# Layer 2 of a four-layer image network: group statistics from one product, shorter chains, and a reordered boundary turn

## The chip, the core and the metric

The kernel runs on one core of a Trainium2 chip. A core has five engines with queues of their own, each in order: TensorE (PE, matrix products and transposes, result in PSUM), VectorE (DVE), ScalarE (ACT), GpSimd (POOL) and SyncE (SP, which here issues all DMAs). They wait for each other through semaphores. The metric is the device time of one execution in microseconds (us), lower is better.

## The reference

Sixteen images of 64 x 64 tokens with 256 channels pass four layers, each `x + layer(group_norm(x))`. All numbers are 32-bit floats. What matters here:

```python
def _gn(v, G=32, eps=1e-5):              # statistics over a whole image and 8 channels
    g = v.reshape(B_, H_, W_, G, C_ // G)
    m = jnp.mean(g, axis=(1, 2, 4), keepdims=True)
    s = jnp.var(g, axis=(1, 2, 4), keepdims=True)
    return ((g - m) / jnp.sqrt(s + eps)).reshape(v.shape)

# layer 1, in part: two maps (mean and max over channels) and a 7x7 convolution of them
feat = jnp.concatenate([jnp.mean(xc, -1, keepdims=True), jnp.max(xc, -1, keepdims=True)], -1)
s = lax.conv_general_dilated(feat, lsa_w, (1, 1), 'SAME', ...)

# layer 2: an involution, 3x3, 16 groups of weights made from the input itself
r = relu(((x @ Wr + br) - mean) * rsqrt(var + BN_EPS) * gamma + beta)
w = (r @ Ws + bs).reshape(B, H, W, G, KK)[:, :, :, :, None, :]
xi = x @ Wi + bi
xp = jnp.pad(xi, ...)
patches = stack of the 9 shifted copies of xp, reshaped to (B, H, W, G, F // G, KK)
out = jnp.sum(w * patches, axis=-1)

x = x + _L0_conv_ref(_gn(x), ...)        # linear attention
x = x + _L1_conv_ref(_gn(x), ...)        # gates, scan over tokens, batch norm
x = x + _L2_conv_ref(_gn(x), ...)        # involution 3x3
x = x + _L3_conv_ref(_gn(x), ...)        # involution 7x7
```

The group norm ahead of layer 2 needs the mean and variance of the finished layer 1 of an image, and the one ahead of layer 3 those of the finished layer 2.

## The kernel before

The program has three large stages, one for each of layers 0, 2 and 3, and between the first two a scan (layer 1) and a pass for the batch norm's statistics. Channels lie on the partitions, in two halves of 128; an image is cut into 8 chunks of 512 tokens.

**Layer 0** runs over pairs of image and head half, 8 steps each, `n` from 0 to `LAST + 15`; the 16 steps from `LAST` on only drain the pipeline. An automatic scheduler sets the order of instructions on each engine there. In the drain the last image gets its gate (`gate1`, at its end L508 on PE, L512 on ACT, L513 to L517 on DVE), then `mapped` is called for its 8 chunks: `affine` scales a chunk (one half on ACT, L172, one on DVE, L175), eight transposes put it into PSUM (L526, tile `px`, two buffers), and DVE reduces it twice, maximum (L530) and sum (L531). After the maps, DVE builds the convolution's band matrices from the 98 weights (L695, L702, then 14 copies, L709, into `convT`) and PE multiplies them with the maps (`psc`, L718), before the scan begins.

**Layer 2** is a loop of 152 turns (`TURNS`, L1286) whose order on every engine is written by hand (`manual_schedule`). Four jobs run in it, each behind the one before by a fixed number of turns, `LAG = (0, 13, 21, 32)` (L1285): the end of layer 1 for a chunk (`end_of_layer1`: DVE `z` L1058, ACT relu L1067 with sums, POOL add L1071, ACT squares L1078), the projection into the padded image `pad` (`projected`, PE L1124, ACT L1128; after chunk 7 two copies L1135 and L1136 fill the halo line), the involution for four lines, and the centring for layer 3 (`centred`, POOL L857). So the first 21 turns have no involution, and the last 3 have only what follows it.

In one turn with an involution, DVE does `z` and `pf` for another chunk (L1058), then two products `pd` of patches and weights (L1208) and one reduction (L1383). POOL reduces the first product (L1221, L1222). PE does, in this order: weights `pw` (L1155), `pr` of the next chunk (L1145), the addition of the finished sums to the residual `lo` (L1195), nine pairs of transposes `pt` for the next turn's patches `xs` (L1170, each pair evicted by ACT, L1174; after three of them `between` is called), the next residual (L1186), transposes of the finished output (L1234), and the projection (L1124). A **boundary turn**, once for each image, prepares chunk 0 of the next image; there the projection of chunk 7 is placed ahead of `pr`, since all nine pairs of chunk 0 read the image that it completes.

Between these jobs run **chains**, one link at each call of `step()`, three calls in a turn: at the start, in `between`, and between the two products. `norm2` and `norm3` are such chains. Each calls `group_norm`, whose `moments` turns the 8 partial sums and squares of each channel into mean and variance with six small DVE instructions (L113 to L123); a product with `gmat` averages means over groups of 8 channels (`pg`, L134), DVE copies it (L140, L142), three instructions form the deviations (L146 to L148), a second product averages them (`pv`, L151), and L93 (DVE) and L94 (POOL) make the inverse root. `norm2` then scales the layer's weights by it on ACT (`wrs`, `wis`, L1096), multiplies them with the means (`pm`, L1106, PE), and forms two biases on DVE (`b` L1112, `bis` L1114). `norm3` ends with the means spread over all partitions (`pb` L844, copy `gmb` L849). With its empty links `norm2` takes four turns, and its last link, the biases, is at the third call of `step()` in a boundary turn, so in DVE's order between the two products.

SP issues in each turn the loads of the next one, then the stores of the last, then the centring's load. A load or store waits in SP's queue until its tile is free or full.

Of the kernel before, what the change touches and what calls it, by code (L numbers as in the profile page):

```python
# [9 lines left out]
F32 = mybir.dt.float32  # L10
AF = mybir.ActivationFunctionType
# [25 lines left out]
def network(ctx: ExitStack, tc: tile.TileContext, a: dict, out: bass.AP):  # L37
# [33 lines left out]
    mean1 = gconst("mean1", [P, NI, 2])  # L71
# [37 lines left out]
    def moments(mv, sums, squares, base, shift):  # L109


        t = small.tile([P, 4], F32, tag="mom", name="mom")
        nc.vector.tensor_reduce(t[:, 0:2], sums, AX.X, ALU.add)  # L113
        nc.vector.tensor_reduce(t[:, 2:4], squares, AX.X, ALU.add)
        if base is None:
            nc.vector.tensor_scalar(mv[:, :, 0], t[:, 0:2], 1.0 / NT, None, ALU.mult)
        else:
            nc.vector.scalar_tensor_tensor(
                mv[:, :, 0], t[:, 0:2], 1.0 / NT, base, ALU.mult, ALU.add
            )  # L120
        nc.vector.tensor_tensor(t[:, 0:2], mv[:, :, 0], shift, ALU.add)
        nc.vector.tensor_tensor(t[:, 0:2], t[:, 0:2], t[:, 0:2], ALU.mult)
        nc.vector.scalar_tensor_tensor(  # L123
            mv[:, :, 1], t[:, 2:4], 1.0 / NT, t[:, 0:2], ALU.mult, ALU.subtract
        )

    def group_norm(fill, stats, pool, tag, apart=False, kept=None, negated=None, beside=None):
# [3 lines left out]
        fill(mv, *stats)  # L131
# [3 lines left out]
        if apart:  # L135
            yield
        gm, rstd = kept or [
# [3 lines left out]
        if negated is not None:  # L141
            nc.vector.tensor_scalar(negated, pg[:, 0:2], -1.0, None, ALU.mult)  # L142
        if apart:
            yield
# [7 lines left out]
        after = beside() if beside else None  # L152
        if apart:
            yield
        inv_sqrt(rstd, pv[:, 0:2], GN_EPS)
        if after:
            after()
        yield
        if apart:
            yield  # L160
# [19 lines left out]
    with ExitStack() as st:  # L180
# [71 lines left out]
        def norm0(i):  # L252
            _, gm, rstd = yield from group_norm(aggregated, (st0.pop(i),), sm, "sm")
            nb = small.tile([P, 2], F32, tag="gn_b", name="gn_b")
            nc.vector.tensor_tensor(nb, gm, rstd, ALU.mult)
            nc.vector.tensor_scalar(nb, nb, -1.0, None, ALU.mult)
            gn0[i] = (gm, rstd, nb)
# [225 lines left out]
        def gate1(i):  # L483

            mv, gm, rstd = yield from group_norm(aggregated, (st1.pop(i),), sm, "sm")
# [31 lines left out]
            nc.vector.tensor_copy(mean1[:, i, :], mv[:, :, 0])  # L517

        def mapped(i, ch):

            xc = loaded.pop(("xm", i, ch))
            affine(xc, xc, i)
# [6 lines left out]
            cols = slice(2 + ch * 4, 6 + ch * 4)  # L529
            nc.vector.tensor_reduce(maps[:, 1, i, cols], px, AX.X, ALU.max)  # L530
            nc.vector.tensor_reduce(maps[:, 0, i, cols], px, AX.X, ALU.add)  # L531
# [58 lines left out]
        for n in range(LAST + 16):  # L590
# [54 lines left out]
            for job in work:  # L645
                if job[0] == "xm":
                    mapped(*job[1:])
# [11 lines left out]
    with ExitStack() as st:  # L659
# [22 lines left out]
        convT = sconst("convT", [P, 5, 2, 2, HW])  # L682
        with tc.tile_pool(name="s_conv", bufs=1) as pcv:
            bmask = pcv.tile([P, 7, HW], F32, tag="bmask", name="bmask")
            nc.sync.dma_start(out=bmask, in_=a["bmask"])
            lsa = pcv.tile([P, 7, 7, 2], F32, tag="lsa", name="lsa")
            nc.sync.dma_start(
                out=lsa.rearrange("p i j c -> p (i j c)"), in_=a["lsa_w"].partition_broadcast(P)
            )
            band = pcv.tile([P, 7, 2, HW], F32, tag="band", name="band")  # L690
            term = pcv.tile([P, 7, 2, HW], F32, tag="term", name="term")
            for dj in range(7):
                dst = band if dj == 0 else term
                for c in range(2):
                    nc.vector.tensor_tensor(  # L695
                        dst[:, :, c, :],
                        lsa[:, :, dj, c].unsqueeze(2).broadcast_to([P, 7, HW]),
                        bmask[:, dj, :].unsqueeze(1).broadcast_to([P, 7, HW]),
                        ALU.mult,
                    )  # L700
                if dj:
                    nc.vector.tensor_tensor(band, band, term, ALU.add)  # L702
            nc.vector.memset(convT, 0.0)
            for delta in range(-2, 3):
                for rr in range(2):
                    for r2 in range(2):
                        di = 2 * delta + rr - r2 + 3
                        if 0 <= di < 7:
                            nc.vector.tensor_copy(  # L709
                                convT[rr * HW : (rr + 1) * HW, delta + 2, :, r2, :],  # L710
                                band[rr * HW : (rr + 1) * HW, di, :, :],
                            )

# [162 lines left out]
    with ExitStack() as st:  # L876
# [25 lines left out]
        mvb = bconst("mvb", [P, 2, 2])  # L902
        sb2 = folded(pc, "l2", "L2_mean", "L2_var", "L2_gamma", "L2_beta", "br")
# [143 lines left out]
        def end_of_layer1(i, rc):  # L1047

            if rc == 0:
                st0[i] = [  # L1050
# [110 lines left out]
        def patches(i, rc, between):  # L1161
# [3 lines left out]
            for j in range(3):  # L1165
# [9 lines left out]
                if j == 0:  # L1175
                    between()
# [589 lines left out]
```

## Time and profile before

| | us |
|---|---|
| median of 3 runs (lowest, highest) | 8064.9 (8053.64, 8065.29) |
| the profiled execution | 8044.92 |
| its span, first to last instruction | 8042.9 |

The profiled execution in stretches, in us from the start of its span; the columns of the engines are busy time, "clock" the share of full speed granted to TensorE, DMA the mean busy share of the 16 DMA engines:

| stretch | what runs | us | PE | DVE | ACT | POOL | clock | DMA |
|---|---|---|---|---|---|---|---|---|
| 0 to 3036 | layer 0 | 3036 | 2609.8 | 2261.3 | 1694.8 | 668.5 | 0.93 | 0.44 |
| 3036 to 3061 | maps of the last image | 25 | (see below) | | | | | |
| 3061 to 3167 | convolution of the maps, scan | 106 | 77.8 | 38.4 | 22.2 | 8.1 | 0.55 | 0.02 |
| 3167 to 3355 | batch norm's statistics | 188 | 145.5 | 177.0 | 172.3 | 0.7 | 0.96 | 0.97 |
| 3355 to 3476 | layer 2, turns without involution | 121 | (see below) | | | | | |
| 3476 to 5400 | layer 2, full turns | 1924 | (see below) | | | | | |
| 5400 to 5697 | layer 2, turns without `z` | 297 | 255.7 | 284.2 | 182.2 | 229.4 | 0.93 | 0.59 |
| 5697 to 5760 | last sums, constants and first loads of layer 3 | 63 | 27.4 | 5.0 | 15.0 | 12.4 | 0.53 | 0.71 |
| 5760 to 8043 | layer 3 | 2283 | 1981.7 | 1062.5 | 1276.4 | 455.8 | 0.98 | 0.82 |

A timeline line reads: start, duration, engine, source line, operation, out<-in with shapes, how many are merged, and in brackets the idle time of the engine before it and what ended that. Lines of layer 2's steady turns, from one start of L1383 to the next, give the length of a turn: 16.16 us where no chain has a link on DVE (4874.00 to 4890.16), 17.61 with `moments` of `norm2` (4800.12 to 4817.73), and 22.49 in a boundary turn (4851.51 to 4874.00). Eight turns, one image, take 141.5 us (4748.69 to 4890.16).

### The profile page before, as it was taken

Reading aid. Unit: us, or ns where it says so; the run is one execution under the profiler, and the core shown is the slowest. Engines: PE = TensorE matmul, PEld = TensorE weight load, DVE = VectorE, ACT = ScalarE, POOL = GpSimd, SP = SyncE. Lnnn points to the kernel's source line nnn. Section 1 sums busy time; section 2 is a strip of 40 time slices with the busy share of each in tenths; the row PEclk is TensorE's granted clock in tenths of the full one; section 3 lists DMA queues with packets and bytes.
Section 4 is the critical chain, followed back from the end, with each engine's and each line's share of the span. In section 5 each row is a group of like instructions: output and inputs, shape, how many; then the busy total and the mean of one; then the engine's idle time right before and its main releaser. Section 6 shows DMA issues by size and latency. Waiting matters only on the chain.

```text
span 8042.9 us, 214160 instructions
## 1 busy us (share of the span) xinstructions
PE 6914.4 (86%) x88876; PEld 5169.1 (64%) x88876; DVE 5726.5 (71%) x6802; ACT 4930.7 (61%) x11392; POOL 3050.4 (38%) x2155
## 2 busy tenths in 40 slices
PE   7888888888889976589999999999688888888898
PEld 5666666666666663156666666666577777777777
DVE  6777777777777776789999999999544444444444
ACT  3555555555555553877777777776455555555554
POOL 1222222222222210168888888887312122111112
PEclk9999999999999986899999999999899999999999
DMA  6644444444333333867878788875688888888887
GB/s 220 197 144 137 137 131 139 137 133 140 129 125 121 113 111 120 313 211 259 275 267 278 267 275 278 266 249 201 204 259 256 259 260 259 258 255 259 260 263 238
DMA packets 1075453, 1689.52 MB, mean 210 GB/s; under 512 B 136417, under 2 KB 680626, under 8 KB 1073330
## 3 DMA queue, kind: packets, MB, share of 16 engines
q1 hardware_dynamic: 1074482, 1675.83, 64.3%
q8 instruction: 700, 11.47, 0.6%
q14 instruction: 271, 2.22, 0.1%
HBM read 1228.47 MB, written 469.76 MB: 211 GB/s over the span
## 4 chain that ended last, share of the span: by engine, by line
PE 48%; DVE 23%; issue 11%; ACT 8%; DMA 7%; POOL 2%; SPq 1%; DVEq 0%; POOLq 0%; ACTq 0%
PE pk L1484 13%; PE pa L1550 8%; DVE pd L1208 7%; PE pkv L302 6%; PE py L444 5%; DVE x L1383 4%; PE pq L290 3%; DMA xn<-in_x 2%; PE pr L1451 2%; PE px L1124 2%; PE pt L1170 2%; PE pctx L368 2%; PE po L429 1%; DVE mq L403 1%; DVE x L472 1%
## 5 line engine op out<-in xcount | busy, mean ns | idle before, releaser
L1208 DVE TENSOR_TENSOR pd<-xs,pw 128x4608 f32<-128x4608 f32 x256 | 1261.4, 4947 | 6.4 <-POOL x L1222 4.5
L1484 PE MATMUL pk<-rt,span 64*128 64x176 f32 x12288 | 1170.5, 326 | 62.6 <-issue 55.3
L1494 ACT ACTIVATE wm<-pk,spanb 128x176 f32<-128x176 f32 x2560 | 847.3, 425 | 569.2 <-PE pk L1484 566.6
L1570 POOL TENSOR_TENSOR ex<-ex,rx 128x192 f32<-128x192 f32 (+2 forms) x768 | 437.1, 570 | 1800.8 <-DVE ex L1563 1272.4
L1221 POOL TENSOR_TENSOR pd<-pd 128x2048 f32<-128x2048 f32 (+2 forms) x384 | 1072.4, 2793 | 118.0 <-DVE pd L1208 65.2
L1484 PEld LDWEIGHTS pk<-rt,span 64*128 64x128 f32 x12288 | 959.8, 190 | 143.4 <-issue 85.5
L1563 DVE SCALAR_TENSOR_TENSOR ex<-pa,msk,ex 128x192 f32<-128x192 f32 x704 | 294.3, 418 | 1004.0 <-ACT ex L1562 925.2
L302 PE MATMUL pkv<-wq,xn 128*128 128x256 f32 x4096 | 983.0, 386 | 2.7 <-ACT va L311 1.9
L302 PEld LDWEIGHTS pkv<-wq,xn 128*128 128x128 f32 x4096 | 784.3, 195 | 228.1 <-issue 114.6
L1550 PE MATMUL pa<-wm,xw 126*32 126x48 f32 x45056 | 753.7, 215 | 200.8 <-issue 182.8
L1499 DVE TENSOR_TENSOR wm<-pk,spanb 128x704 f32<-128x704 f32 x896 | 794.0, 888 | 185.7 <-PE pk L1484 183.8
L398 POOL TENSOR_TENSOR qa<-qa,mq 128x1024 f32<-128x1024 f32 x256 | 501.6, 1980 | 1026.4 <-DVE mq L403 512.0
L1550 PEld LDWEIGHTS pa<-wm,xw 126*32 126x32 f32 x45056 | 623.4, 112 | 383.5 <-issue 334.5
L1170 PE MATMUL pt<-ident,pad 128*128 128x128 f32 x4608 | 639.1, 287 | 145.1 <-ACT xs L1174 87.6
L1170 PEld LDWEIGHTS pt<-ident,pad 128*128 128x128 f32 x4608 | 521.7, 146 | 302.4 <-ACT xs L1174 117.6
L1383 DVE TENSOR_REDUCE x<-pd 128x512 f32<-128x4608 f32 x128 | 634.0, 4953 | 4.4
L1174 ACT COPY xs<-pt 128x512 f32<-128x512 f32 x1152 | 588.9, 597 | 37.2 <-PE pt L1170 36.9
L444 PE MATMUL py<-wo,o 128*128 128x256 f32 x2048 | 542.4, 422 | 64.3 <-ACT va L311 59.6
L444 PEld LDWEIGHTS py<-wo,o 128*128 128x128 f32 x2048 | 496.0, 310 | 108.8 <-ACT va L311 76.7
L290 PE MATMUL pq<-xn,wq 128*128 128x512 f32 x1024 | 533.1, 637 | 33.4 <-ACT xn L165 21.1
L1562 ACT ACTIVATE ex<-pa,msk 128x192 f32<-128x192 f32 x704 | 300.2, 426 | 373.3 <-PE pa L1550 185.3
L1124 PE MATMUL px<-x2p,wis 128*128 128x512 f32 x1024 | 467.9, 599 | 11.8 <-DMA x2p<-x_d 8.1
(243 smaller groups left out, 11893.5 us busy)
## 6 DMA issues: line engine op xcount, KB each, us to landing
xw<-strips SPq DMA_DIRECT2D x1408, 256.0 KB
xn<-in_x SPq DMA_DIRECT2D x256, 512.0 KB
x_d<-x SPq DMA_DIRECT2D x256, 512.0 KB
strips<-cen SPq DMA_DIRECT2D x352, 256.0 KB
xin<-in_x SPq DMA_DIRECT2D x128, 512.0 KB
x<-in_x SPq DMA_DIRECT2D x128, 512.0 KB
xm<-x_d SPq DMA_DIRECT2D x128, 512.0 KB
x2p<-x_d SPq DMA_DIRECT2D x128, 512.0 KB
```

The costliest lines, as they stand in the source:

```text
L290: nc.tensor.matmul(pq, lhsT=wq[:, h, f0 : f0 + P], rhs=xn[:, h], start=(h == 0), stop=(h == 1),)
L302: nc.tensor.matmul(pkv[:, q], lhsT=xn[:, h, q * P : (q + 1) * P], rhs=wq[:, h, f0 + P : f0 + 384], start=(h == 0), stop=(h == 1),)
L444: nc.tensor.matmul(py[:, q, :], lhsT=om[i, hf][:, :, ch * 4 + q], rhs=wo[:, hf, :], start=(hf == 0), stop=(hf == 1),)
L1124: nc.tensor.matmul(px, lhsT=w[:, h, fh * P : (fh + 1) * P], rhs=x2[:, h], start=(h == 0), stop=(h == 1),)
L1170: nc.tensor.transpose(pt[:, k, h * P : (h + 1) * P], lines[:, h, rc * 4 + e + k, 2 * j : 2 * j + P], ident,)
L1208: nc.vector.tensor_tensor(pd.rearrange("p r (g f) k -> p r g f k", f=16), run, pw.rearrange("p r (g k) -> p r g k", k=9).unsqueeze(3).broa ...
L1221: nc.gpsimd.tensor_tensor(pd[..., 0:n], pd[..., 0:n], pd[..., n : 2 * n], ALU.add)
L1383: nc.vector.tensor_reduce(x3[:, :, P:C], pd1, AX.X, ALU.add)
L1484: nc.tensor.matmul(pkv[:, b, m], lhsT=span[half, first + gg, s0 : s0 + P], rhs=rto[half, o // 4 * 2 + m, :], start=True, stop=True,)
L1494: nc.scalar.activation(dst[:, m // 2, m % 2], pkv[:, m // 2, m % 2], AF.Identity, bias=spanb[:, g0 + m : g0 + m + 1],)
L1499: nc.vector.tensor_tensor(dst, pkv, spanb[:, g0 : g0 + 4].rearrange("p (b m) -> p b m", b=2).unsqueeze(3).broadcast_to([P, 2, 2, NTL]), AL ...
L1550: nc.tensor.matmul(pav[p0 : p0 + 32, :, tj * TC : (tj + 1) * TC].rearrange("c g (w v) -> c g w v", v=2), lhsT=xw[0:TILE_IN, k, tj, 32 * q ...
```

## The change

**Layer 2, statistics.** Sums and squares of a chunk go into one tile of 128 x 32. One product with `gsum` (`gmat` divided by the number of tokens, made once) sums them over the group, and one DVE reduction of the PSUM tile over the chunks gives mean and mean square. `moments`, the copies of `pg`, the deviations and the second product are gone, as is `mean1`, which layer 0 kept for it.

**Layer 2, chains.** New chains start at the end of the turn in which the last squares are taken, with the product at once. `norm2` does its DVE instructions and POOL's power at the next start of a turn, the scaling on ACT in `between`, the product `pm` at the third call, and the biases at the start of the turn after. `norm3` likewise, with `pb` at the third call. `LAG` becomes (0, 10, 18, 28) and the loop has 148 turns.

**Layer 2, boundary turn.** The pairs of transposes for lines 2 to 5 of the chunk come first, the projection of chunk 7 after six pairs, and the three pairs that read the halo line last.

**Layer 0, drain.** From step `LAST` on, a chunk's second half is scaled on POOL in place of DVE, and two of the four sums over channels are taken by ACT (`accum_out`).

**Convolution bands.** `convT` comes ready from the host, one load of 128 x 1280; L695 to L709 are gone. On SP it stands ahead of the last four loads `xm`.

```diff
-    def moments(mv, sums, squares, base, shift):
-        t = small.tile([P, 4], F32, tag="mom", name="mom")
-        nc.vector.tensor_reduce(t[:, 0:2], sums, AX.X, ALU.add)
-        nc.vector.tensor_reduce(t[:, 2:4], squares, AX.X, ALU.add)
...
-            nc.vector.tensor_copy(mean1[:, i, :], mv[:, :, 0])
-
-        def mapped(i, ch):
+        def mapped(i, ch, shared):
             xc = loaded.pop(("xm", i, ch))
-            affine(xc, xc, i)
+            if shared:
+                nc.scalar.activation(
+                    xc[:, 0], xc[:, 0], AF.Identity,
+                    bias=ab[:, 1, i, 0:1], scale=ab[:, 0, i, 0:1],
+                )
+                nc.gpsimd.tensor_scalar(
+                    xc[:, 1], xc[:, 1], ab[:, 0, i, 1:2], ab[:, 1, i, 1:2], ALU.mult, ALU.add
+                )
+            else:
+                affine(xc, xc, i)
...
-            nc.vector.tensor_reduce(maps[:, 1, i, cols], px, AX.X, ALU.max)
-            nc.vector.tensor_reduce(maps[:, 0, i, cols], px, AX.X, ALU.add)
+            c0, k = 2 + ch * 4, 2 if shared else 0
+            nc.vector.tensor_reduce(maps[:, 1, i, c0 : c0 + 4], px, AX.X, ALU.max)
+            nc.vector.tensor_reduce(maps[:, 0, i, c0 + k : c0 + 4], px[:, k:4], AX.X, ALU.add)
+            for q in range(k):
+                sq = wk.tile([P, C], F32, tag="sq", name="sq", bufs=1)
+                nc.scalar.activation(
+                    sq, px[:, q], AF.Copy, accum_out=maps[:, 0, i, c0 + q : c0 + q + 1]
+                )
...
-                    mapped(*job[1:])
+                    mapped(*job[1:], n >= LAST)
...
-        convT = sconst("convT", [P, 5, 2, 2, HW])
-        with tc.tile_pool(name="s_conv", bufs=1) as pcv:
...
+        convT = sconst("convT", [P, 5, 2, 2, HW], a["conv"])
...
+        gsum = bconst("gsum", [P, P])
+        nc.vector.tensor_scalar(gsum, gmat, 1.0 / NT, None, ALU.mult)
...
+                st0[i] = wk.tile([P, 2, 2, NCH], F32, tag="st0", name="st0")
+            sums, squares = st0[i][:, 0], st0[i][:, 1]
...
+        def group_moments(stats):
+            pg = tr.tile([P, CT], F32, tag="tr", name="pg")
+            nc.tensor.matmul(
+                pg[:, 0 : 4 * NCH], lhsT=gsum, rhs=stats.rearrange("p k h c -> p (k h c)"),
+                start=True, stop=True,
+            )
+            yield
+            t = small.tile([P, 4], F32, tag="mom", name="mom")
+            nc.vector.tensor_reduce(
+                t, pg[:, 0 : 4 * NCH].rearrange("p (n c) -> p n c", c=NCH), AX.X, ALU.add
+            )
+            return t[:, 0:2], t[:, 2:4]
+
+        def deviation(rstd, squares, shift):
+            v = small.tile([P, 2], F32, tag="gn_d", name="gn_d")
+            nc.vector.tensor_tensor(v, shift, shift, ALU.mult)
+            nc.vector.scalar_tensor_tensor(v, squares, GN_EPS, v, ALU.add, ALU.subtract)
+            nc.gpsimd.tensor_tensor(rstd, v, mhalf[:, 0:2], ALU.pow)
+
         def norm2(i):
+            m, sq = yield from group_moments(st0.pop(i))
             ngm2[i] = wk.tile([P, 2], F32, tag="ngm2", name="ngm2", bufs=4)
-            _, gm, rstd = yield from group_norm(
-                moments, (*st0.pop(i), mean1[:, i], ngm1[:, i]), tr, "tr", apart=True,
-                negated=ngm2[i],
-            )
+            nc.vector.tensor_tensor(gm, m, ngm1[:, i, :], ALU.subtract)
+            nc.vector.tensor_tensor(ngm2[i], ngm1[:, i, :], m, ALU.subtract)
+            deviation(rstd, sq, m)
+            yield
...
-            yield
-            yield
             yield
             pm = tr.tile([P, CT], F32, tag="tr", name="pm")
...
-        def patches(i, rc, between):
+        def patches(i, rc, between, late):
...
+            pairs = [(j, e) for j in range(3) for e in (0, 2, 4)]
+            if late:
+                pairs.sort(key=lambda p: p[1] == 0)
+            for n, (j, e) in enumerate(pairs):
+                if late and n == 6:
+                    late()
...
         def norm3(i):
+            m, sq = yield from group_moments(st3.pop(i))
+            nc.vector.tensor_copy(gm3[:, i, :], m)
+            d = small.tile([P, 2], F32, tag="gn_s", name="gn_s")
+            nc.vector.tensor_tensor(d, m, ngm2.pop(i), ALU.add)
+            deviation(rs3[:, i, :], sq, d)
+            yield
+            yield
+            gmb[i] = wk.tile([P, C], F32, tag="gmb", name="gmb", bufs=2)
+            after = spread_means(i, tr, "tr", gmb[i])
+            yield
+            after()
...
-        LAG = (0, 13, 21, 32)
-        TURNS = NI * NCH + 24
+        LAG = (0, 10, 18, 28)
+        TURNS = NI * NCH + 20
...
                 step()
-                for c in begun:
-                    next(c)
-                chains.extend(begun)
-                begun.clear()
...
                 first = nxt and not nxt[1]
-                if first:
-                    relus()
-                    projected(*proj)
-                    ahead = prepare(lambda: None)
-                elif nxt:
-                    ahead = prepare(relus)
+                if nxt:
+                    ahead = prepare(first and (lambda: projected(*proj)))
...
                     sums_on_pool(pd, x3)
                 step()
+                for c in begun:
+                    next(c)
+                chains.extend(begun)
+                begun.clear()
                 if inv:
                     pd1 = products(1, w1, now[3])
```

## The prediction

> **What bounds the kernel now.** The costliest groups come first:
>
> ```profile
> span 8042.9 us, 214160 instructions
> ...
> L1208 DVE TENSOR_TENSOR pd<-xs,pw 128x4608 f32<-128x4608 f32 x256 | 1261.4, 4947 | 6.4 <-POOL x L1222 4.5
> ...
> L1383 DVE TENSOR_REDUCE x<-pd 128x512 f32<-128x4608 f32 x128 | 634.0, 4953 | 4.4
> ```
>
> Layer 2's products and reduction wait only 10.8 us in 1895. Next, windows around the change (length, then busy us of PE, PEld, DVE, ACT, POOL; clock, DMA share, GB/s):
>
> ```profile
> 3036.00:3061.00 25.00, 14.21 (x64) 11.94 (x64) 24.07 (x28) 7.34 (x9) 0.00 (x0) 0.57 0.27 84
> 3355.00:3476.00 121.00, 56.71 (x209) 30.71 (x210) 38.43 (x61) 91.22 (x218) 60.71 (x47) 0.72 0.75 245
> 3476.00:5400.00 1924.00, 1745.66 (x9458) 1174.96 (x9457) 1835.53 (x890) 1469.15 (x3320) 1614.65 (x774) 0.98 0.78 263
> ```
>
> The full turns are DVE's: busy 1835.5 of 1924. What it waits for there (total, times, longest):
>
> ```profile
> DVE b L1112 <- PE pm L1106: 73.4, 13, 5.9
> ```
>
> A 14th, of 6.8, comes at 5432: 80.2 us in all. One such turn on DVE, then on PE:
>
> ```profile
> 4851.51 4.95 DVE L1383 TENSOR_REDUCE x<-pd 128x512 f32<-128x4608 f32 x1
> 4856.38 1.25 DVE L1058 SCALAR_TENSOR_TENSOR z<-x,ngm,pf 128x512 f32<-128x512 f32 x1
> ...
> 4858.33 4.95 DVE L1208 TENSOR_TENSOR pd<-xs,pw 128x4608 f32<-128x4608 f32 x1
> 4868.77 0.27 DVE L1112 TENSOR_SCALAR b<-pm,sb 64x1 f32<-64x1 f32 x1 [5.50 <-PE pm L1106]
> ```
>
> ```profile
> 4867.41 1.00 PE L1106 MATMUL pm<-gn_m,wis 128*128 128x1 f32 x8
> 4868.34 0.39 PE L1106 MATMUL pm<-gn_m,wrs 128*64 128x1 f32 x4
> 4868.66 3.04 PE L1170 MATMUL pt<-ident,pad 128*128 128x128 f32 x24
> 4871.54 1.04 PE L1186 MATMUL lo<-ident,x2r 128*128 128x128 f32 x8
> 4872.41 1.04 PE L1234 MATMUL pt<-ident,x 128*128 128x128 f32 x8
> ...
> 4879.01 3.33 PE L1195 MATMUL lo<-x,ident 128*128 128x512 f32 x4 [2.85 <-DVE x L1383]
> ```
>
> PE reaches `pm` only behind the projection, `pr`, `lo` and three pairs, so the second product stands 5.5 us behind the bias. An undisturbed turn from L1383 to L1383 lasts 16.16 (3 x 4.95 + 2 x 0.75, less overlaps); POOL works 15.1 of it (2 x 1.28 + 2.36 + 8.55 + 1.67), PE 15.3, ACT 13.5. So at most 1 us per turn can be gained by DVE before POOL or PE decides, and the gain must come from the turns above 16.16.
>
> **Part by part.** All sums are against the profiled execution, 8044.9 (span 8042.9); the median, 8064.9, lies 20 higher and is moved by the same amount.
>
> *A, maps and convolution: -16.* The link between layer 0 and the scan:
>
> ```profile
> 3059.28 1.21 DVE L531 TENSOR_REDUCE maps<-px 128x4 f32<-128x1024 f32 x1
> ...
> 3061.84 1.09 DVE L702 TENSOR_TENSOR band<-band,term 128x896 f32<-128x896 f32 x1
> ```
>
> `psc` starts at 3066.80, 6.4 after the last map (3060.41), behind `term`, `band` and nine copies. With the band built by the host only L714 (0.46) is left: -5.9; `psc`'s 8.6 of PE stays, and outlasts DVE's and ACT's preparations beside it (7.6). The load `convT` (640 KB) is issued some 29 us ahead and lands long before; in SP's queue it passes four `xm` loads, some 2 us at 266-395 GB/s, in their slack of 3. Eight chunks of maps took 24.5 us, DVE 2.8 each (2 x 1.13 + 0.54). Afterwards DVE does 1.7 (1.13 + 0.57), ACT 1.95 (0.73 + 2 sums like L453's 0.42 + 0.19), PE 1.94 at its half clock. POOL's new `affine` has no row of its form: between L1071's 1.13-1.28 (128x512) and L398's 1.98 (128x1024); I take 1.2, its own size. With two PSUM buffers 2.1-2.3 a chunk, 18.5: -6. The previous image's eight chunks in the drain -2; the gate's chain, in which L702 and `term` wedge themselves between L147 and L148 (0.6 and 1.05 late), -2.1; the copies that leave before the gate gain nothing, since POOL's memset L666 (3.51) stands before its first `affine`. Bounds: -8 (chunks gain nothing) to -20.
>
> *B, three fewer turns before the first involution: -14.* The head before the first involution, on DVE:
>
> ```profile
> 3393.65 0.75 DVE L1058 SCALAR_TENSOR_TENSOR z<-x,ngm,pf 128x512 f32<-128x512 f32 x1 [1.72 <-DMA pf<-fac_d]
> ...
> 3398.76 0.75 DVE L1058 SCALAR_TENSOR_TENSOR z<-x,ngm,pf 128x512 f32<-128x512 f32 x1 [3.50 <-DMA pf<-fac_d]
> ...
> 3406.30 0.75 DVE L1058 SCALAR_TENSOR_TENSOR z<-x,ngm,pf 128x512 f32<-128x512 f32 x1 [6.00 <-DMA pf<-fac_d]
> ```
>
> The loads of `pf` set its pace: four turns from 3387.66 to 3411.26, 5.9 each. Three go, -17.7. But three more turns with `z` now have an involution as well, 16.5 instead of the last turns' 15.3: +3.6. Bounds -18 (the three later cost nothing, as turns that POOL paces anyway) to -5 (the same bytes must cross in less time, so that half of the 17.7 is waited for elsewhere).
>
> *Tail: -4 (0 to -8).* One turn less after the last L1383 (5692), and POOL's memsets for layer 3 (L1412, 3.65) no longer stand before the last centring, so the first loads of layer 3, issued behind its stores, move up.
>
> *C, chains of fewer DVE instructions: -30.* `norm2` took DVE 2.76 us per image outside the biases (1.31 + 0.14 + 0.98 + 0.07 + 0.26), `norm3` 2.84 (1.32 + 0.07 + 1.05 + 0.40). Now one reduction and three or four small ones: some 1.31 and 1.40. Of the 1.45 saved, 0.38 goes back: an early `z` runs against L1222, as above, 1.25 for 0.75. That is -1.07 x 28 links = -30. Bounds -45 (1.45 and no more contention, 28 links) to -20. The sums over groups go to PE for all chunks at once, in one product `pg` of 32 columns: no more than the 0.39 of four products in the row `pm`; the wait for it is a rival below.
>
> The Trainium skill, "SBUF — State Buffer", section "Who interferes with whom", says that a VectorE instruction with two SBUF inputs and a GpSimd instruction reading SBUF lock each other out. The 1.25 above beside L1222 agrees; strictly applied, each shortened link would give back all of its gain at `z`, and C would be 0.
>
> *D, the boundary wait: -55.* Halo line's patches come last and `pm` behind the patches; the biases move from between the products to the next turn's start. `pm` ended 17.2 us after L1383's start (4868.73 - 4851.51). Now six pairs, `lo` and `pt` (3.04 + 1.04 + 1.04 = 5.1) are ahead of it, the scaling of weights on ACT, which paces the pairs, lies in this turn (1.3), and the late projection waits for a PSUM tile (0.5, estimated by a copy's 0.59): 24.1. The two halo copies (2 x 0.32) were in the turn already. DVE asks for it after the turn (16.2), a link (1.1) and L1383 (4.95): 22.3. The stall becomes 1.8: 80.2 - 14 x 1.8 = 55. Behind it wait `z`, then ACT's relu and POOL's additions (1.3 us of slack after POOL's 15.1), and the next first product; its patches are evicted at some 21.8, in time. Bounds: -75 (stall 0.4) to 0 (as long as before).
>
> *Nothing:* moved stores and loads. The windows show 263 GB/s at a share of 0.78; 1.07 times that is needed, and the batch norm's stage moved 359-395. `x3` is now stored and read in the same turn: SP waits the landing (5.4 by the centring's loads) with some 12 of slack; uncovered it would be 5.4 in each of 128 turns at the worst, which I give no share of the range, since the next turn's loads stand ahead of the stores in SP's queue.
>
> Sum: -16 - 14 - 4 - 30 - 55 = -119. Execution 7925.9; median 7945.9.
>
> **Rivals.**
>
> *R1, the wait keeps its size and only moves* to the next turn's start, where ACT sets the pairs' pace and PE, idle 2.85 behind L1383, is slow again (L1195 3.33 beside 1.99). For it: ACT's 13.5 plus scaling and halo is near the turn. Against: 17.2 + 7 leaves 5 us until 29. D = 0: 8064.9 - 64 = 8001.
>
> *R2, the chains wait for their products at the start of a turn*, since `pg` comes at the end of the last and DVE wants it 4.95 later. PE's `px` ends 3.1 into the turn in the trace, `pg` 0.4 later, so 1.5 is left; in the turn after a boundary PE is late. If each of 28 links waits 1.5: +42, 7988.
>
> *R3, slower:* PE at half clock through the boundary turn and the one after. The late projection stops PE for a PSUM tile and for ACT. Price: `px` +3.4, pairs +1.5, `lo` and `pt` +1.7, `pm` +1.1, the next turn's `weights`, `pr` and `lo` +3.7: 11.4 x 14 = +160, so 8064.9 - 119 + 160 = 8106. It decides once the boundary wait exceeds 10 us (1.8 + 119 / 14). Against: the clock is 0.98 over the full turns, and the slow instructions follow gaps of 2.9 only.
>
> The Trainium skill, "TensorE: Matmul & The Clock Gate", section "What's actually happening", lets TensorE fall back to half clock after an idle window of about 3.4 us. The trace has the slow `lo` after 2.85; by the rule a boundary turn with gaps of 1-3 would keep its clock, by the row part of R3 (+1.3 x 14 = 18) could come.
>
> **How the numbers follow.** Forecast 0.60. Its own range takes D from -40 to -70 (stall 2.9 to 0.7) and the other terms half of the way to their bounds: -12 - 9.5 - 2 - 25 - 40 = -88.5, or 7976, and -18 - 16 - 6 - 37.5 - 70 = -147.5, or 7917. R1 0.22, R2 0.10, R3 0.05, and 0.03 that one new wait eats just the whole gain. The whole range goes from all terms at their far ends (-20 - 18 - 8 - 45 - 75 = -166: 7899) to R1 with the other terms half of the way to their near ends (-12 - 9.5 - 2 - 25 = -48.5: 8016); R2 lies inside. About 0.2%, or 16 us, is what a measurement here tells from no change: faster 0.93 (forecast, R1, R2 and a little), same 0.02, slower 0.05.
>
> **What shows it.** Right: boundary turns of 18-19.5 instead of 22.5, the others 16.2-17.2; the wait for `pm` under 3 us, now at a turn's start ahead of `z`; `psc` within 1 us of the last map and some 16 us earlier; the first L1383 some 33 earlier, near 3443; three rows gone from each chain. Wrong: DVE waiting for `pg` (R2); waits for `xs` or `pw` at L1208 after a boundary; a clock under 0.95 in the full turns (R3); SP waiting for `x3` so long that `x2r` comes late.

## The result, and the profile after

| | before | after |
|---|---|---|
| median (lowest to highest), us | 8065.09 (8053.64 to 8084.54), 4 runs | 7971.36 (7969.65 to 7973.67), 4 runs |
| ratio, 95% interval | | 0.9882 (0.9862 to 0.9901) |
| span of the profiled execution | 8042.9 | 7969.2 |

The kernel became 1.2% faster. The costliest groups of the page of after, for the same two lines of layer 2:

```profile
L1185 DVE TENSOR_TENSOR pd<-xs,pw 128x4608 f32<-128x4608 f32 x256 | 1256.0, 4947 | 5.5 <-POOL x L1199 5.3
...
L1357 DVE TENSOR_REDUCE x<-pd 128x512 f32<-128x4608 f32 x128 | 634.0, 4953 | 4.4
```

The work of these lines is what it was (4947 and 4953 ns each); what changed lies between them. Windows of after, in the same columns as before: the last image's maps, the head of layer 2, the full turns:

```profile
3034.00:3058.00 24.00, 15.75 (x64) 12.66 (x64) 14.48 (x16) 12.64 (x38) 6.08 (x8) 0.50 0.34 108
3345.00:3466.00 121.00, 62.76 (x210) 33.08 (x211) 32.17 (x62) 81.97 (x195) 54.52 (x43) 0.72 0.63 213
3466.00:5310.00 1844.00, 1669.50 (x9323) 1125.68 (x9322) 1801.79 (x709) 1456.40 (x3310) 1599.11 (x773) 1.00 0.82 274
```

The maps have given 9.6 us of DVE to ACT and POOL and yet take as long (24 against 25); the head moves 213 GB/s where it moved 245; in the full turns DVE is busy 97.7% instead of 95.4%. What DVE still waits for there (total, times, longest):

```profile
DVE b L1085 <- PE pm L1079: 30.9, 13, 4.9
```

A boundary turn of after on DVE, on PE and on ACT:

```profile
4265.34 4.95 DVE L1357 TENSOR_REDUCE x<-pd 128x512 f32<-128x4608 f32 x1
4272.20 0.27 DVE L1085 TENSOR_SCALAR b<-pm,sb 64x1 f32<-64x1 f32 x1 [1.91 <-PE pm L1079]
```

```profile
4262.95 3.70 PE L1097 MATMUL px<-x2p,wis 128*128 128x512 f32 x8 [2.65 <-ACT xs L1151]
4267.78 1.53 PE L1147 MATMUL pt<-ident,pad 128*128 128x128 f32 x12 [1.13 <-ACT pad L1108]
...
4271.77 0.39 PE L1079 MATMUL pm<-gn_m,wrs 128*64 128x1 f32 x4
```

```profile
4264.97 0.69 ACT L1101 ACTIVATE pad<-px,bis 128x512 f32<-128x512 f32 x1 [1.11 <-PE px L1097]
4266.69 0.69 ACT L1101 ACTIVATE pad<-px,bis 128x512 f32<-128x512 f32 x1 [1.03 <-PE px L1097]
...
4268.47 1.57 ACT L1151 COPY xs<-pt 128x512 f32<-128x512 f32 x3 [0.53 <-PE pt L1147]
```

This turn began with L1357 at 4248.08, so `pm` ends at 24.1 (4272.16) and DVE, free at 4270.29, stands 1.9. The late projection is a relay: PE waits for ACT's evictions (2.65), ACT for PE's two halves (1.11 and 1.03), PE for the halo copies (1.13), ACT for the transposes (0.53). Each engine is idle in the other's share.

Where the 73.7 us between the two spans lie, by anchors taken from the rows (the last gate's end, `psc`, the first `z`, the first and last L1383/L1357, the first `wm` of layer 3), with a second profile of each kernel from the experiments below:

| profile | span | last gate to end of `psc` | first `z` to first L1383 | first to last L1383 | end of `psc` to first `wm` |
|---|---|---|---|---|---|
| before | 8042.9 | 45.4 | 93.8 | 2216.0 | 2682.6 |
| before, again (b_again) | 8049.9 | 45.9 | 94.1 | 2206.9 | 2671.9 |
| after | 7969.2 | 40.3 | 89.2 | 2138.7 | 2595.6 |
| after, again (a_again) | 7940.3 | 37.4 | 86.1 | 2136.3 | 2592.1 |

By the means of two: maps and convolution -6.8, head -6.3, turns with an involution -74, the rest of the stretch from `psc` to `wm` about -3 (the end behind the last L1383 -5, the batch norm's stage +2), together -90. The two ends of the program, which the edits hardly touch, spread by more than several of these terms: up to the last gate's end 3032 and 3038 before, 3019 to 3034 in the profiles of the changed kernel and its variants; layer 3 from its first `wm` 2282.7 and 2293.9 before, 2303.1 and 2284.5 after. So the steps are judged by the stretch from `psc` to `wm`, not by the spans.

### The profile page after: what moved, and what is told of

It reads as the page before. It is cut to its first block, busy times and chain, and to the rows that moved or that the text cites. A ratio compares the mean times of both kernels' runs of the same rounds, so it can differ in the third digit from the quotient of the medians.

```text
span 7969.2 us, 213876 instructions
## 1 busy us (share of the span) xinstructions
PE 6865.4 (86%) x88812; PEld 5137.4 (64%) x88812; DVE 5671.4 (71%) x6527; ACT 4934.1 (62%) x11456; POOL 3053.4 (38%) x2171
## 4 chain that ended last, share of the span: by engine, by line
PE 46%; DVE 23%; issue 12%; ACT 8%; DMA 7%; POOL 3%; SPq 1%; DVEq 0%; POOLq 0%; ACTq 0%
PE pk L1458 13%; DVE pd L1185 9%; PE pa L1524 8%; PE pkv L270 5%; PE py L412 5%; DMA xn<-in_x 2%; PE pq L258 2%; PE pr L1425 2%; DVE x L1357 2%; PE pctx L336 2%; PE px L1097 1%; DVE mq L371 1%; ACT sq L421 1%; DVE z L1008 1%; DVE mq L378 1%
## 5 line engine op out<-in xcount | busy, mean ns | idle before, releaser
L1185 DVE TENSOR_TENSOR pd<-xs,pw 128x4608 f32<-128x4608 f32 x256 | 1256.0, 4947 | 5.5 <-POOL x L1199 5.3
L1147 PE MATMUL pt<-ident,pad 128*128 128x128 f32 x4608 | 604.6, 280 | 146.0 <-ACT xs L1151 122.7
L1147 PEld LDWEIGHTS pt<-ident,pad 128*128 128x128 f32 x4608 | 505.3, 142 | 294.1 <-ACT xs L1151 145.9
L1357 DVE TENSOR_REDUCE x<-pd 128x512 f32<-128x4608 f32 x128 | 634.0, 4953 | 4.4
L1151 ACT COPY xs<-pt 128x512 f32<-128x512 f32 x1152 | 584.4, 597 | 17.5 <-PE pt L1147 17.4
```

The source lines that it names most:

```text
L1147: nc.tensor.transpose(pt[:, k, h * P : (h + 1) * P], lines[:, h, rc * 4 + e + k, 2 * j : 2 * j + P], ident,)
L1151: nc.scalar.copy(xs[:, e : e + 2, j, :], pt)
L1185: nc.vector.tensor_tensor(pd.rearrange("p r (g f) k -> p r g f k", f=16), run, pw.rearrange("p r (g k) -> p r g k", k=9).unsqueeze(3).broa ...
L1357: nc.vector.tensor_reduce(x3[:, :, P:C], pd1, AX.X, ALU.add)
```

## The experiments

**b_again and a_again**, both kernels as they are.

> The kernel before, unchanged, a second profile. From layer 3's first `wm` on DVE to the end, its profile took 2282.7 us (5760.2 to 8042.9) and that of the changed kernel 2303.1 (5666.1 to 7969.2), with the same instructions. Theory: this is a spread between executions of one program, and the first profile was a short one: this time 2290 to 2310, span 8050 to 8075, while the stages up to the last L1383 agree with the first profile within 2 us. Rival: the change lengthens layer 3 (other places of buffers, another start of its queue): then 2280 to 2286 again, span 8041 to 8047.

> The changed kernel, unchanged, on the chip of the next three. The stages that no edit touches spread between executions (start to the end of layer 0's last gate 3019 to 3038, layer 3 from its first `wm` 2280 to 2299); the stretch from the end of `psc` to the first `wm` of layer 3, 2595.6 in its profile, should come again within 4 us, boundary turns 18.4. Against the next kernel's order (projection first) it should be some 0.4% slower, 25 to 40 us. Rival: the 58 us by which the order with the projection first came out shorter were mostly the spread, then under 15 us.

Layer 3 took 2293.9 in the second profile of before, between the two kernels' first ones: the 14 us by which the end after the last L1357 seemed to have grown (2350.5 to 2364.8) are a spread of executions. The other half of the expectation failed: the last L1383 was reached 4 us earlier, and four boundary turns of before lasted 21.1 instead of 22.4 to 22.8. The second profile of after agrees in the stretch (2592.1), and its ratio is 0.9874 (0.9855 to 0.9893).

What sets these 21.1 apart is the clock granted to TensorE. In layer 2 of the traces it falls to 0.5 for stretches of 3.41 us or a multiple of that. Of the first 13 boundary turns of each profile, the long ones are those that such a stretch touches, without an exception (lengths of turns as above; for after and no_late, which comes next, of the turn that holds the wait of `b`):

| profile | with a stretch at half clock | without |
|---|---|---|
| before | 13: 22.4 to 22.8 | 0 |
| before, again | 9: 22.4 to 22.8 | 4: 21.1 |
| after | 3: 19.9 to 21.4 | 10: 18.4 |
| after, again | 2: 20.0 and 21.5 | 11: 18.4 |
| no_late | 7: 17.3 to 17.5 | 6: 16.7 |
| no_late_b | 6: 17.3 to 17.4 | 7: 16.6 to 16.7 |

**no_late and no_late_b**: the boundary turn's projection ahead of `pr` again, pairs in their old order, all else as changed.

```diff
                 def prepare(late):
-                    relus()
+                    if not first:
+                        relus()
...
-                if nxt:
-                    ahead = prepare(first and (lambda: projected(*proj)))
+                if first:
+                    relus()
+                    projected(*proj)
+                if nxt:
+                    ahead = prepare(None)
```

> The changed kernel with the boundary turn's projection placed ahead of `pr` again and the pairs in their old order; chains and lags as changed. Theory: the halo line's place at the end of the turn is worth the time that PE else waits for ACT's evictions and halo copies, 1.4 + 0.6 us, and these come on top of the wait of `b`: 1.5 to 2.5 in each of 14 boundary turns, +20 to +35: 7991 to 8006. Rival: `pm` waits for the amount of work ahead of it, which is the same in both orders, and the order is worth nothing: 7966 to 7976.

> The kernel with the projection first in the boundary turn, unchanged, on the chip of the next three. Stretch from the end of `psc` to the first `wm` of layer 3: 2565.8 in its first profile, again within 4 us; ratio to before 0.983 to 0.986. Rival: its lead over the changed kernel (2595.6 and 2592.1 in two profiles) was the spread: then above 2580.

Measured: 7916.79 (7913.22 to 7926.27), ratio 0.9841 (0.9826 to 0.9855), and again 7933.10, ratio 0.9846 (0.9824 to 0.9868); stretch 2565.8 and 2566.0. The theory was wrong in sign, and the rival's nothing was wrong too: the halo line's place at the end doesn't save time, it costs some 28 us of the stretch, and this kernel has the lowest ratio of the study (in the second pair the intervals of the two ratios overlap; the stretches of both pairs agree). A boundary turn of no_late at full clock on ACT, PE and DVE (its reduction, L1361 there, began at 4225.19):

```profile
4233.52 1.24 ACT L1101 ACTIVATE pad<-px,bis 128x512 f32<-128x512 f32 x2
```

```profile
4229.25 3.65 PE L1097 MATMUL px<-x2p,wis 128*128 128x512 f32 x8
...
4246.20 0.39 PE L1079 MATMUL pm<-gn_m,wrs 128*64 128x1 f32 x4
```

```profile
4247.30 0.26 DVE L1085 TENSOR_SCALAR b<-pm,sb 64x1 f32<-64x1 f32 x1
```

PE projects while ACT waits for `z` and takes its relu, so both halves are ready and are evicted back to back (1.24, no idle time ahead of them). `pm` ends at 21.4 instead of 24.1, before DVE asks at 22.1: no wait. Such turns last 16.7 (18.4 in after). In the seven that a stretch at half clock touches, `pm` ends at 23.0, DVE waits 0.8 to 1.0, and they last 17.3 to 17.5; these are all the waits of `b` in the full turns, 6.1 us against 30.9.

**nl_old_bias**: no_late with the biases back between the products, by one `yield` fewer in `norm2`; the scaling and `pm` thereby come one call of `step()` earlier too.

```diff
             deviation(rstd, sq, m)
-            yield
             wrs = wk.tile([P, 2, 64], F32, tag="wrs", name="wrs")
```

> Projection first in the boundary turn, and one link of `norm2` fewer: scaling of weights at the turn's start, `pm` after three pairs, biases between the products again, as in the kernel before. Theory: what took the boundary wait away is the place of the biases at the next turn's start; now `pm` again ends some 17 us after L1357's start, while DVE asks for it at 12: waits of 5 to 6.5 in each of 14 boundary turns, stretch from `psc` to `wm` 2566 + 70 to 90. Rival: the short chains alone bring it (the new scaling comes early enough): under +15.

Measured: 7966.99 (one run), stretch 2594.4, +28.5 (turns with an involution +33, head -6); neither the theory's 70 to 90 nor the rival's 15. The wait on DVE was 2.6, not 5 to 6.5:

```profile
4666.16 0.27 DVE L1084 TENSOR_SCALAR b<-pm,sb 64x1 f32<-64x1 f32 x1 [2.62 <-PE pm L1078]
```

The rest of the old wait belonged to the old chain. In before its scaling of weights stood on ACT in the turn ahead of the boundary; PE's last pairs waited for it and were then slow (2.82 for twelve transposes, 1.63 elsewhere):

```profile
4849.12 2.82 PE L1170 MATMUL pt<-ident,pad 128*128 128x128 f32 x12 [2.66 <-ACT xs L1174]
```

so that PE began the boundary turn's projection at 6.5 after L1383's start (4857.99), and at 4.1 in nl_old_bias and no_late (4229.25). The clock has a part in it: in the four boundary turns of b_again that kept it whole the projection began at 5.1 and DVE waited 4.1 instead of 5.4 to 5.9. A chain with fewer links takes both away by itself: of -83 in the stretch (mean 2677.3 to 2594.4) none needs the new place of the biases. That place, with the scaling and `pm` that move along, is worth a further -28.5 by this one profile, and the late projection costs +28: in the change as made the two cancel (2594.4 against 2595.6 and 2592.1).

**lag11**: after with LAG (0, 11, 19, 29) and one turn more.

> The changed kernel with LAG (0, 11, 19, 29) and one turn more: `pm` and the scaling of weights fall into the turn ahead of the boundary turn. Theory: the wait of `b` for `pm` (26.4 us in 13 full boundary turns, 15.7 and 5.9 in the head) came from these links lying in the boundary turn; it goes to under 5 us in all, boundary turns from 18.4 to 16.7, that is -22; the head gives back 21.6 and pays one turn of 6: -15 at most, 0 at least. Time 7935 to 7950. Rival: the wait only changes its name (the first product waits for patches that the late projection delays): 7962 to 7972.

Measured: 7947.72 (7945.77 to 7950.78), ratio 0.9878 (0.9862 to 0.9895), stretch 2590.5, of which the head 86.2 with one turn more. The median lies in the theory's range, but before, too, was faster beside it (8049.8); the ratio and the stretch are those of after. The theory's mechanism came by half: waits of `b` in the full turns halved (15.2 us, 9.7 of it in four turns that a stretch at half clock touches) and the boundary turn itself is 16.65. The gain went elsewhere, and not to the first product as the rival had it: the turn after the boundary, 17.5 in after, is now 18.8, since a link of `norm3` stretches there from 0.16:

```profile
4559.09 1.62 DVE L1052 TENSOR_TENSOR gn_d<-gn_s 128x2 f32<-128x2 f32 x1
```

Eight turns take 136.3 as before. The head's further turn cost nothing that shows (86.2 beside 89.2 and 86.1). A variant with LAG (0, 13, 21, 31), meant to show what three turns of the head cost, deadlocks and gave no time.

**a_escale**: after with the scaling moved from between the pairs to the boundary turn's start (the first `yield` behind the scaling instead of ahead of it).

> The changed kernel, late projection kept, with the scaling of weights at the boundary turn's start on ACT. Theory: of the 2.65 that PE waits for `xs` ahead of the late projection, 1.3 is the scaling (1.33 on ACT); `pm` then ends at 24.1 - 1.3 = 22.8 after L1357's start, DVE wants it at 22.2: boundary turns 18.4 to 17.1, -1.3 x 14 = -18, stretch from `psc` to `wm` 2572 to 2580. Rival: the halo wait (1.1) and the projection in the turn's middle are what counts, and ACT's squares take the gap over: under -6.

Measured: 7948.94 (one run), stretch 2586.6, -7, of which the head -4; boundary turns 18.4 to 18.6. ACT, then PE:

```profile
4518.94 0.35 ACT L1070 ACTIVATE wrs<-wr,gn_r 128x64 f32<-128x64 f32 x1 [2.84 <-POOL gn_r L1054]
```

```profile
4522.64 0.66 PE L1147 MATMUL pt<-ident,pad 128*128 128x128 f32 x4 [1.56 <-ACT rt L1121]
```

ACT's idle time at the start was no hole: the weights wait for POOL's inverse root as long as the relu waits for `z`, so the 1.3 is still ahead of the pairs: PE now waits for `rt` (1.56) instead of `xs`, and begins the late projection 14.8 into the turn, as in after. Its relay is as it was (ACT waits 1.25 and 1.03 for the halves). A stretch at half clock touches 12 of the 13 boundary turns here, but the one without lasted 18.4 as well. What the scaling alone costs this run does not tell, since it is ahead of `pm` in both places.

**nl_cen_first**: no_late with POOL's centring ahead of its two additions.

> Projection first in the boundary turn, and POOL's centring put ahead of its two additions in every turn. In plain turns (16.64) POOL's loop decides: `z` 1.24 beside L1199, then ACT's relu, then 1.57 of idle POOL, then 2 x 1.28 + 2.37 + 10.2. Theory: centring fills the idle 1.57, sums start as soon as the first product is there, and plain turns fall to 16.2 to 16.4: -0.25 to -0.4 in some 100 turns, -25 to -40, stretch from `psc` to `wm` near 2535. Rival, by the same lock that lengthens `z`: the centring now runs beside `z` and `pf`, both take 1.2 or more, and turns get 0.3 to 1 longer: +30 to +100.

Measured: 8117.01 (8108.8 to 8126.99), ratio 1.0077 (1.0057 to 1.0096), slower than before; plain turns 18.5. DVE and POOL, side by side:

```profile
4075.22 2.73 DVE L1008 SCALAR_TENSOR_TENSOR pf<-x,ngm,pf 128x512 f32<-128x512 f32 x1
```

```profile
4074.60 2.80 POOL L807 TENSOR_TENSOR cen<-xc,gmb 128x1024 f32<-128x1024 f32 x1
```

The rival's mechanism, at a higher price than it named (+1.9 a turn, stretch +188): `pf` (0.75 alone) waits for the whole of POOL's instruction and ends 0.55 behind it. The Trainium skill ("SBUF — State Buffer", "Who interferes with whom") says of the contention for the port pair that the two engines share that "it's an exclusive lock"; these rows agree, and so does `cen`, which began while `z` still ran and took 2.80 instead of 2.37.

**nl_nocen**: no_late; POOL centres one quarter of the channels for layer 3, zeros are stored for the other three.

> Projection first in the boundary turn, and POOL centres a quarter of the channels for layer 3 (the other three quarters are left out, zeros are stored in their place): POOL's work in a turn 15.1 - 1.7 = 13.4. Theory: POOL's loop through the lock on `z` sets the plain turns of 16.64; without it `z` is 0.75 again and they last 16.16 (3 x 4.95 + 2 x 0.75, less overlaps): -0.48 in some 100 turns, stretch from `psc` to `wm` 2566 - 40 to -55. Rival: DVE's own work is 16.6 whatever POOL does: under -10.

Measured: 7930.95 (one run), stretch 2555.3, -10.5; plain turns 16.53 instead of 16.64. Theory wrong, rival about right: POOL now idles 1.5 ahead of its sums, and `z` is still slow:

```profile
4305.04 1.12 DVE L1011 SCALAR_TENSOR_TENSOR z<-x,ngm,pf 128x512 f32<-128x512 f32 x1
```

```profile
4303.97 1.65 POOL L1202 TENSOR_TENSOR x<-pd 128x512 f32<-128x512 f32 x1
```

POOL's sums (8.54 + 1.65 = 10.2) start with the end of the first product and outlast the second product and the reduction (9.9), so in a turn in which DVE has no wait `z` meets their last instruction, with the centring or without.

**nl_noshare**: no_late with the drain's maps scaled and summed as before.

> Projection first, and the maps of the drain computed as before (half of a chunk scaled on DVE, both sums on DVE). From the end of the last gate to the start of `psc`: 34.6 in the profile of before, 28.9 in those of the changed kernels, of which the host's bands gave 4.6 (6.3 to 1.7 after the last map). Theory of step A: sharing the maps is worth 6 of the 16 forecast, so 34 to 35 here. Rival: the loads of `xm` (2 us apart, waiting for their tiles) and POOL's memset ahead of its first half pace the eight chunks, and sharing gives 1: 29 to 31.

Measured: 7951.95 (one run), last gate to start of `psc` 29.4, against 28.9, and to its end 39.8, against 40.2. Sharing brings 0.5 at the most, and nothing up to the end; a_again's 27.0 to the start shows how far single profiles spread. ACT's group of sums in after, with what ended its idle time:

```profile
L510 ACT ACTIVATE sq<-px 128x256 f32<-128x256 f32 x15 | 5.7, 378 | 8.4 <-DVE maps L507 8.2
```

ACT's two sums do not run beside DVE's, they wait for its last one (8.2 us in five waits); a chunk's tile is then held for 1.9 of DVE and 1.1 of ACT in a row, longer than DVE's two full passes held it (2 x 1.2).

**nl_best**: no_late with the scaling at the turn's start, `gsum` on ACT, and the memset of `r` placed after the exponentials in the program.

> Projection first, and three waits removed that the profiles showed: the scaling of weights on ACT moved from between the pairs (where PE waits 2.0 to 2.7 for `xs`) to the turn's start (where ACT idles 2.8 for `z`); `gsum` made by ACT, since on DVE it stood 7.7 behind POOL's memset of `pad`; the memset of `r` moved behind the exponentials, since `ab` on DVE took 3.0 beside it. Theory: all boundary turns 16.7 (now 16.7 and 17.4 in turn, -5), head -5 (79.7 in the run that scaled early, 85.2 here), batch norm's stage -2, last gate to `psc` -2 to -3: together -12 to -15 against the run before this, stretch from `psc` to `wm` 2551 to 2556. Rival: each gap is refilled by the next wait, under -5.

Measured: 7938.88 (7935.36 to 7955.5), ratio 0.9854 (0.9839 to 0.9869), stretch 2568.4: the rival. The head gained 1.7 to 2.9, but boundary turns became 17.7, because POOL's additions, 1.3 later by the scaling, push its sums into `pf`:

```profile
4532.09 2.02 DVE L1008 SCALAR_TENSOR_TENSOR pf<-x,ngm,pf 128x512 f32<-128x512 f32 x1
```

```profile
4531.35 2.21 POOL L1199 TENSOR_TENSOR x<-pd 128x512 f32<-128x512 f32 x1
```

`gsum` off DVE changed nothing in the batch norm's stage (from `psc`'s end to the first `z` 306.8, and 306.1 to 307.0 in after and no_late; 305.0 and 303.1 in before), so what made it 2 us longer stays open. The scheduler left `r`'s memset where it had been; that edit tested nothing.

## Why the prediction was right, and where it was not

The forecast of 7946 was 25 us too low, the direction and most of the loop's sum right. Of the -119, -90 shows in the profiles (means of two for each kernel): A -7 for -16, B -2 for -14, tail -5 for -4, C -31 for -30, D -44 for -55. The loop's other idle time (-3) and the batch norm's stage (+2) had no term.

*D, the boundary wait, -55.* DVE's waits for `pm` between the first and the last reduction went from 80.2 to 32.2, -48 (in the second profiles from 71.5 to 30.8). In ten of after's 13 full boundary turns the chain of times held to a tenth: `pm` at 24.1 forecast and measured, DVE's demand at 22.3 and 22.2, a stall of 1.8 and 1.9; the other three, at half clock, stalled 3.5 to 4.9. That the sum came out so well is luck, for two of its terms were wrong by as much in opposite directions. Its start, `pm` at 17.2, held the old chain's scaling and the half clock of before; with the new chain and `pm` in its old place it is 14.9 (nl_old_bias). And the step that failed is "the late projection waits for a PSUM tile (0.5)": the projection's own halves, evictions and halo copies were counted nowhere, as "in the turn already", though at the turn's end nothing covers them. They cost 2.7 (24.1 against 21.4). I took the new order as part of the gain; by no_late it costs 28 of the stretch, and without it no stall is left where the clock is whole.

*C, shorter chains, -30.* This came, by DVE's rows between the first and the last reduction (each instruction counted to the start of the next, idle time left out; means of two profiles). The chains' instructions fell from 81.0 to 35.1, -46 where 28 x 1.45 = 41 was forecast; `z` rose from 92.5 to 109.8, of which 2.6 are three more of them, so 14.7 where 28 x 0.38 = 11 was forecast. (The far bound of -45 is more than its own terms give, 41.) Where the 0.5 at `z` falls was read too narrowly. The "undisturbed" 16.16 of before stands behind a boundary wait, in which POOL had caught up; in after every plain turn is 16.64, with `z` beside POOL's last sum, four turns of an image where before had two:

```profile
4066.65 1.24 DVE L1008 SCALAR_TENSOR_TENSOR z<-x,ngm,pf 128x512 f32<-128x512 f32 x1
```

```profile
4065.70 1.65 POOL L1199 TENSOR_TENSOR x<-pd 128x512 f32<-128x512 f32 x1
```

The prediction charged this 0.5 to the shortened links; it falls on the plain turns between them. On the other side, it did not see that shorter chains clear PE in the turn ahead of the boundary.

*B, the head, -17.7 (before +3.6 in later turns).* First `z` to first L1383 shrank by 4.6, and 6.3 by the means. The nine turns up to the boundary's `z` took 60.4 us where before twelve took 73.1, so three turns did go, at 4.2 each rather than 5.9. The rest was eaten by the first boundary turn, in which no product covers PE and ACT:

```profile
3436.94 0.75 DVE L1008 SCALAR_TENSOR_TENSOR z<-x,ngm,pf 128x512 f32<-128x512 f32 x1 [1.40 <-DMA pf<-fac_d]
...
3454.21 0.27 DVE L1085 TENSOR_SCALAR b<-pm,sb 64x1 f32<-64x1 f32 x1 [15.73 <-PE pm L1079]
```

That turn, from its `z` to the first product, took 19.0; before 10.8. The bound of -5, which I gave to the bytes of the loads, was the right size by another cause. Of the later turns' +3.6, DVE's rows show +4.6 (109 of `z` and `pf` instead of 106, 0.87 and 0.67 each), so that of B some -2 is left.

*A, -16.* Gate to `psc`'s end shrank by 5.1 and by 6.8 in the means. The bands came as forecast (`psc` 1.7 behind the last map instead of 6.3). The -6 for sharing the maps was wrong: the step "afterwards DVE does 1.7, ACT 1.95" took the engines as working beside each other.

*Tail, -4.* Last L1383 to first `wm`: 67.8 to 61.7 and 63.4.

*The rivals.* R1 fell: the wait did not keep its size. R2 fell in the full turns, where no wait for `pg` shows; in the head there were two (3.4 and 3.1). R3 fell in its sum: the clock over the full turns is 1.00, above before's 0.98, and half clock touched three of after's 13 boundary turns, which cost 6 us. But what was held against it, slow instructions only behind gaps of 2.9, was misread: in before the row at 4849.12 is slow after 2.66, and half clock touches all 13 boundary turns there, 1.3 to 1.7 each beside the 21.1 of whole clock, some 20 us. So some 14 of D's gain are the clock's, which no term of the sum held.

## What to carry to other kernels

When two edits aim at one wait, undo each alone: here a shorter chain and the new place of a dependent instruction removed it, and the reordering that came with them cost as much as the second gave. A producer and a consumer that evict in turns belong where another engine covers both; moved behind that cover, their relay is paid in full. Removing a stall also removes the slack that other engines had used to catch up, so count what runs beside what in the turns that become regular. Where turns of one kind come in two lengths, read the granted clock of each before looking for another cause.

## What the hardware showed

POOL's and DVE's instructions on two SBUF operands hold each other up: a `z` or `pf` of 0.75 became 1.24, 2.02 or 2.73 by where POOL stood, and each time ended 0.54 to 0.55 behind POOL's instruction. A DVE `tensor_scalar` with one SBUF operand did the same beside a POOL memset (`gsum`, 128x128, 7.67 beside 7.58; `ab`, 128x2, 3.03 beside 3.51).

PE was slow after one idle time of 2.66 (transposes 2.82 for 1.63, before) and not after one of 2.65 (`px` 3.70, 3.60 elsewhere, after). The length of the gap alone does not tell; the traces suggest what does, though no run varied it. In layer 2 of each trace all stretches at half clock begin on one grid with steps of 3.41 us. Before's gap lay for 2.3 of its 2.66 in one step of its grid, after's was split between two, 1.8 and 0.8 (columns as in the windows above: us, PE, PEld, DVE, ACT, POOL, clock, DMA):

```profile
4845.37:4848.78 3.41, 1.09 (x10) 0.80 (x8) 3.41 (x2) 3.38 (x10) 3.41 (x2) 1.00 1.06 373
4848.78:4852.19 3.41, 3.07 (x15) 3.07 (x16) 3.38 (x2) 2.63 (x6) 3.33 (x2) 0.50 1.08 375
```

```profile
4258.71:4262.12 3.41, 1.59 (x13) 1.23 (x12) 3.41 (x2) 3.38 (x10) 3.41 (x2) 1.00 0.97 357
4262.12:4265.53 3.41, 2.58 (x6) 1.25 (x7) 3.38 (x2) 2.30 (x5) 3.33 (x2) 1.00 1.07 372
```

PE was busy 0.32 of the step ahead of the half clock, and 0.47 and 0.76 of the two that kept the clock. In the full turns of before, 19 of the 22 stretches at half clock follow a step in which PE was busy at most 0.43, and no step under 0.44 went without one; in a_escale, though, all 12 follow a step of 0.54 to 0.55, so the share is not the whole of it.
